# Attention's four weight products by quarters, seven for eight

## The chip, the core and the metric

The kernel runs on one core of a Trainium2 chip. A core has five engines that work side by side, each on its own queue of instructions in order: TensorE (matrix products, PE in the profile, with its weight loads as PEld), VectorE (DVE), ScalarE (ACT), GpSimd (POOL) and SyncE (SP, which here only issues DMAs). They share an on-chip memory of 128 partitions (SBUF); the matrix products land in a second memory (PSUM) of eight banks, each with 512 float32 values in every partition, and VectorE or ScalarE takes them from there. The metric is the device time of one execution in microseconds (us).

## What is computed

A layer on 4 x 2048 tokens of 256 features, all float32: linear attention with a decay inside chunks of 32 tokens, a layer norm, a gated feed-forward with integer weights, and another layer norm.

```
Q = x @ W_q.T;  K = x @ W_k.T;  V = x @ W_v.T          # D = 256, chunks of 32 tokens
decay = sigmoid(log_decay[0])
mask[i, j] = decay ** (i - j) if i >= j else 0          # 32 x 32
S = (Qc @ Kc.T) * mask;  O = S @ Vc                     # inside each chunk
out = (sigmoid(x @ W_g.T) * O) @ W_o.T + x
x = layernorm(x + out)
h = silu(x @ wg.T / 127) * (x @ wu.T / 127)             # hidden 768, integer weights
x = layernorm(x + h @ wd.T / 127)
```

The kernel uses Q K^T = x (W_q^T W_k) x^T: it forms the 256 x 256 product `m_sb` once, and per block y = x m, and then the scores from x and y. So a block of tokens meets four float32 weight matrices of 256 x 256 in attention: `m_sb`, `wg`, `wv` and `wo`.

## The kernel before

The 8192 tokens are cut into 16 blocks of 512 (`TB`). x comes in twice: transposed (`xT`, features on partitions, 2 x 128, with the 512 tokens along the row) for the products, and as it is (`xn`) for the residual. A tile that is "feature-major" has features on partitions and tokens along the row; "token-major" is the other way round, with the block's four groups of 128 tokens (`NG` = 4) side by side.

The attention of block n:
- `attn_y` (matmul L320, copy by VectorE L327) makes `yT`, feature-major: two output tiles of 128 x 512, each the sum of two products over the two halves of the features.
- `attn_gate` (L304, sigmoid by ScalarE L311) makes `sg` in the same shape.
- `attn_v` (L339, copy by ScalarE L346) makes `v`, token-major: for each group of 128 tokens two products with the 128 x 256 halves of `wv`; two groups share a bank.
- `attn_scores` (L359) forms the scores from x and y in pieces of 64 tokens, and VectorE masks them into `sT` (L369).
- `attn_values` (L380) forms the products of v and `sT`; VectorE multiplies them by the gate into `goT` (L387), feature-major.
- `attn_out` multiplies `goT` by `wo` in `project_back` (L406, named pa), VectorE adds twice x from PSUM (L427), and `layer_norm` (L264 to L288) writes h.

The feed-forward of block b then needs h feature-major and as two parts, a rounded one (`hT_hi`, float32r) and a rest (`hT_lo`, float16). `move_h` turns h by 32 x 32 transposes on VectorE (L461) and 16 small DMAs; `split_h` makes the parts on ScalarE (L484) and VectorE (L485). `ffn_up` runs over six chunks of 128 hidden features (L502): sigmoid on ScalarE (L510), two products on VectorE (L512, L514), then `u_hi` on ScalarE (L521) and `u_lo` on GpSimd (L522). `ffn_down` multiplies all of these by the weights in `project_back` (L406, named fdn), VectorE adds h (L529), and `finish` normalizes and stores.

A loop over b = 0 to 13 joins the two: the attention of block n = b + 2 stands beside the feed-forward of block b. In the order of the program: load xT and xn of n, `attn_y`, `attn_gate`, `attn_v`, `attn_scores`, `move_h` of b + 1, `ffn_up` half 0, `attn_values`, `split_h` of b + 1, `ffn_up` half 1, `attn_out` of n, `ffn_down` and `finish` of b, and a look at some of the integer weights (`look_up`, L230). Before the loop stand the attention of blocks 0 and 1, y of block 2, and the conversion of the integer weights to float32r and float16 (`integers`, L217) by ScalarE; behind it the feed-forward of the last two blocks.

The framework sets the semaphores and the queue order of each engine when the kernel is built. The order of the program gives precedence, but an instruction whose inputs are late may be passed: in the trace, the copy of `yT` stands between instructions of the layer norm of the block before. `tc.keep_in_program_order` holds single instructions to the program's order on their engine (the conversions and the split are held so). The order is fixed from then on. All eight PSUM banks belong to one pool (`bank`): a product takes a free bank and gives it back when the last reader is done.

Of the kernel before, what the change touches and what calls it, by code (L numbers as in the profile page):

```python
# [38 lines left out]
F32 = mybir.dt.float32  # L40
# [6 lines left out]
P = 128  # L47
# [4 lines left out]
NG = TB // P  # L52
SCALE = 1.0 / 127.0
# [8 lines left out]
def kernel(  # L62
# [30 lines left out]
    acts = ctx.enter_context(tc.tile_pool(name="acts", bufs=H // P + 3))  # L93
    small = ctx.enter_context(tc.tile_pool(name="small", bufs=8))
# [41 lines left out]
    if NB > 1:  # L136
        xns[1] = load_xn(1)
    ffn_int = [
        load_w(nc.sync, w, name)
        for w, name in ((ffn_gT, "fg_int"), (ffn_uT, "fu_int"), (ffn_dT, "fd_int"))  # L140
# [73 lines left out]
    def integers(w_int, name, dtype):  # L214
        name = f"{name}_{'hi' if dtype == F32R else 'lo'}"
        t = const.tile(list(w_int.shape), dtype, tag=name, name=name)
        tc.keep_in_program_order(nc.scalar.copy(t, w_int))  # L217
        return t


    halves = [
        (w_int, slice(i * w_int.shape[1] // 2, (i + 1) * w_int.shape[1] // 2))
        for w_int in ffn_int
        for i in range(2)
    ]
    top = const.tile([P, len(halves)], F32, tag="top", name="top")

    def look_up(i):
        w_int, ks = halves[i]
        reduced = nc.vector.tensor_reduce(  # L230
            top[:, i : i + 1],
            w_int[:, ks, :].rearrange("p k n -> p (k n)"),
            mybir.AxisListType.X,
            ALU.max,
            apply_absolute_value=True,
        )
        tc.keep_in_program_order(reduced)

    def count_wide():

        wide = const.tile([P, len(halves)], F32, tag="wide", name="wide")
        nc.vector.tensor_scalar(wide, top, EXACT, None, ALU.is_gt)
        ones = const.tile([P, 1], F32, tag="ones", name="ones")
        nc.vector.memset(ones, 1.0)
        pw = bank("pw")
        nc.tensor.matmul(pw[:1, : len(halves)], lhsT=ones, rhs=wide, start=True, stop=True)
        count = const.tile([1, 1], F32, tag="count", name="count")
        nc.vector.tensor_reduce(count, pw[:1, : len(halves)], mybir.AxisListType.X, ALU.add)
        n_wide = const.tile([1, 1], I32, tag="n_wide", name="n_wide")
        nc.vector.tensor_copy(n_wide, count)  # L250
        return n_wide
# [45 lines left out]

    def attn_gate(b):
        xt = xTs[b]
        sg = work.tile([P, KD, TB], F32, tag="sg", name=f"sg_{b}")  # L300
        for dc in range(KD):
            pg = bank(f"pg_{b}_{dc}")
            for ec in range(KD):
                nc.tensor.matmul(  # L304
                    pg,
                    lhsT=wg[:, ec, dc * P : (dc + 1) * P],
                    rhs=xt[:, ec, :],
                    start=(ec == 0),
                    stop=(ec == KD - 1),
                )  # L310
            nc.scalar.activation(sg[:, dc, :], pg, AF.Sigmoid)  # L311
        return sg

    def attn_y(b):
        xt = xTs[b]
        yT = work.tile([P, KD, TB], F32, tag="yT", name=f"yT_{b}")
        for fc in range(KD):
# [12 lines left out]
    def attn_v(b):  # L330
        xt = xTs[b]
        v = work.tile([P, NG, D], F32, tag="v", name=f"v_{b}")
        per = TB // D
# [40 lines left out]
    def attn_values(b, sT, v, sg):  # L374
        goT = work.tile([P, KD, TB], F32, tag="goT", name=f"goT_{b}")
        for dc in range(KD):
# [10 lines left out]
            nc.vector.tensor_tensor(goT[:, dc, :], po, sg[:, dc, :], ALU.mult)  # L387
        return goT

    def back_terms(g, parts, ws):  # L390


        pairs = list(zip(parts, ws))[:: -1 if g % 2 else 1]
        return [(part[k], w[:, k, :]) for part, w in pairs for k in range(len(part))]
# [26 lines left out]
    def attn_out(b, goT, up=H_UP):  # L421
        xn = xns.pop(b)
        r = norm.tile([P, NG, D], F32, tag="h", name=f"h_{b}")

# [6 lines left out]
        project_back(b, (chunked(goT),), (wo,), residual, "pa")  # L431
# [92 lines left out]
    def ffn_down(b, uT, h):  # L524
# [8 lines left out]
        project_back(b, uT, fd, residual, "fdn")  # L533
# [26 lines left out]
    if second:  # L560
        sT_second = attn_scores(second, ys.pop(second))
    hs[first] = attn_out(first, goT, 1 if NB == 1 else H_UP)
    fg, fu = (
        [integers(w, name, dtype) for dtype in (F32R, F16)]
        for w, name in zip(ffn_int, ("fg", "fu"))
    )
    if second:
        goT = attn_values(second, sT_second, v_second, sg_second)
    if NB > 2:
        xTs[2] = load_xT(2)  # L570
        ys[2] = attn_y(2)
    if second:
        hs[second] = attn_out(second, goT, 1 if NB == 2 else H_UP)
    fd = [integers(ffn_int[2], "fd", dtype) for dtype in (F32R, F16)]
# [5 lines left out]
    for b in range(NB - 2):  # L580
# [5 lines left out]
        uT = [], []  # L586
        yT = ys.pop(n) if n in ys else attn_y(n)
# [9 lines left out]
        if looked < len(halves):  # L597
            look_up(looked)
            looked += 1
    for i in range(looked, len(halves)):  # L600
        look_up(i)
# [70 lines left out]
    for g in range(NG):  # L672
        pb = bank(f"fdn_{last}_{g}")[:, :D]
        terms = back_terms(g, uT_last, fd)
# [31 lines left out]
    def wide_block(start, weights):  # L706
# [18 lines left out]
        for hc in range(KH):  # L725
            pg = bank(f"fg_w_{hc}")
            pu = bank(f"fu_w_{hc}")
            for pb, w in ((pg, wide_g), (pu, wide_u)):
                for dc in range(KD):
                    nc.tensor.matmul(  # L730
                        pb,
                        lhsT=w[:, dc, hc * P : (hc + 1) * P],
# [15 lines left out]
        project_back("w", (uT,), (wide_d,), residual, "fdn")  # L748
# [3 lines left out]
        n_wide, min_val=0, max_val=len(halves) * P, skip_runtime_bounds_check_because="a count"  # L752
    )
    with tc.If(wide_any > 0):
        weights = []
        for w_int in ffn_int:
            t = w_int.bitcast(F32)
            nc.vector.tensor_scalar(t, w_int, SCALE, None, ALU.mult)
            weights.append(t)
# [44 lines left out]
```

## Time and profile before

| What | Value |
|---|---|
| Time, median of 3 runs | 549.88 us (549.49 to 552.0) |
| Profiled execution: time, span | 549.92 us, 548.2 us |
| Mean granted TensorE clock | 0.995 |
| One block in the loop | 33.1 us |
| ACT_TABLE_LOAD (before sqrt and before sigmoid), each | 1283 ns |
| u_lo on POOL, 128x512 | 1280 ns |
| u on VectorE, 128x512 | 691 ns |
| sg, v on ScalarE from PSUM, 128x512 | 597, 588 ns |
| yT copy on VectorE, 128x512 | 671 ns |
| Integer conversion on ScalarE, 128x1536 | 1455 to 1470 ns |
| Largest waits: POOL for u_hi; VectorE (sT) for ps; ScalarE (s) for fg | 405.0, 78.2, 76.1 us |

The span runs from the first to the last instruction; the time is that of the device for the same execution and contains 1.7 us more. A wait in the last row is idle time of the engine that waits, in total over the span. Durations of matmuls in the groups overlap each other, so that the lengths in the chain of waits, where they don't, are the ones to add.

### The profile page before, as it was taken

To read this page: it belongs to the slowest core of one execution; us is meant where nothing else is said; L and a number is where in the kernel's file an instruction comes from. 1 tells how busy PE (TensorE), PEld (TensorE's weight loads), DVE (VectorE), ACT (ScalarE), POOL (GpSimd) and SP (SyncE) were. 2 spreads that over 40 slices of the span, in tenths; PEclk is the share of its full clock that TensorE was granted. 3 is DMA by queue.
4 is the path that set the end of the run, shared out by engine and by line. 5 is a ranking of instruction groups with operands and counts; after the bars stand their busy time and mean duration, and the time that the engine had idled before them with its cause. 6 is when DMAs were issued, how large, how long until landed. Compare 5 with 4: busy or idle time off the path is not lost.

```text
span 548.2 us, 8472 instructions
## 1 busy us (share of the span) xinstructions
PE 538.8 (98%) x3150; PEld 387.6 (71%) x3150; DVE 385.3 (70%) x956; ACT 231.3 (42%) x383; POOL 128.6 (23%) x122
## 2 busy tenths in 40 slices
PE   8999999999999999999999999999999999999994
PEld 5677767767667686677857677676676867678793
DVE  4267784859768486794848758496784858848875
ACT  2217524336243352433435243452433425344745
POOL 2000412305022040321304022050221404123453
PEclk9999999999999999999999999999999999999997
DMA  7431214121221312214122231213213120020102
GB/s 256 168 113 50 67 45 110 39 71 45 89 66 39 84 54 77 58 42 112 40 64 52 70 85 39 74 43 94 62 39 93 62 62 16 8 71 1 38 2 80
DMA packets 41996, 36.77 MB, mean 67 GB/s; under 512 B 4576, under 2 KB 37344, under 8 KB 41952
## 3 DMA queue, kind: packets, MB, share of 16 engines
q1 hardware_dynamic: 40832, 35.15, 22.5%
q10 hardware_dynamic: 1088, 1.05, 0.6%
q8 instruction: 26, 0.43, 0.3%
q14 instruction: 18, 0.15, 0.1%
q0 software_dynamic: 32, 0.00, 0.0%
HBM read 20.45 MB, written 8.39 MB: 53 GB/s over the span
## 4 chain that ended last, share of the span: by engine, by line
PE 97%; DVE 1%; ACT 1%; issue 0%; POOL 0%; DVEq 0%
PE fg L502 16%; PE fu L502 16%; PE fdn L406 15%; PE pg L304 10%; PE pa L406 10%; PE pv L339 10%; PE py L320 10%; PE po L380 5%; PE ps L359 3%; PE pi L148 1%; ACT r L646 0%; PE pt L443 0%; PE pm L162 0%; ACT L273 0%; ACT rstd_f L273 0%
## 5 line engine op out<-in xcount | busy, mean ns | idle before, releaser
L522 POOL TENSOR_TENSOR u_lo<-u,u_hi 128x512 f16<-128x512 f32 (+1 forms) x102 | 123.9, 1216 | 409.5 <-ACT u_hi L521 405.0
L510 ACT ACTIVATE s<-fg 128x512 f32<-128x512 f32 (+1 forms) x102 | 58.1, 570 | 76.2 <-PE fg L502 76.1
L512 DVE SCALAR_TENSOR_TENSOR s<-fg,s 128x512 f32<-128x512 f32 (+1 forms) x102 | 66.7, 654 | 28.0 <-ACT s L510 27.8
L521 ACT CAST u_hi<-u 128x512 fp32r<-128x512 f32 (+1 forms) x102 | 60.4, 592 | 48.8 <-DVE u L514 48.3
L514 DVE TENSOR_TENSOR u<-fu,s 128x512 f32<-128x512 f32 (+1 forms) x102 | 67.1, 660 | 13.8 <-POOL u_lo L522 1.1
L502 PE MATMUL fg<-hT_hi,fg_hi 128*128 128x512 f32 (+1 forms) x204 | 71.5, 431 | 0.0
L369 DVE TENSOR_TENSOR sT<-ps,mask 64x256 f32<-64x256 f32 x32 | 13.5, 422 | 78.5 <-PE ps L359 78.2
L502 PE MATMUL fu<-hT_hi,fu_hi 128*128 128x512 f32 (+1 forms) x204 | 61.4, 382 | 0.0
L502 PE MATMUL fg<-hT_lo,fg_lo 128*128 128x512 f16 (+1 forms) x204 | 58.9, 369 | 0.0
L304 PE MATMUL pg<-xT,wg 128*128 128x512 f32 x128 | 58.2, 598 | 0.0
L339 PEld LDWEIGHTS pv<-wv,xT 128*128 128x128 f32 x256 | 48.6, 190 | 13.4 <-issue 7.7
L502 PE MATMUL fu<-hT_lo,fu_lo 128*128 128x512 f16 (+1 forms) x204 | 58.1, 366 | 0.0
L406 PE MATMUL pa<-wo,goT 128*128 128x256 f32 x256 | 58.0, 379 | 0.0
L339 PE MATMUL pv<-wv,xT 128*128 128x256 f32 x256 | 57.9, 379 | 0.0
L320 PE MATMUL py<-xT,m_sb 128*128 128x512 f32 x128 | 57.6, 593 | 0.0
L406 PE MATMUL fdn<-fd_hi,u_hi 128*128 128x256 f32 x360 | 55.2, 295 | 0.0
L406 PEld LDWEIGHTS pa<-wo,goT 128*128 128x128 f32 x256 | 48.5, 190 | 7.6 <-DVE rstd_a L286 0.2
L406 PEld LDWEIGHTS fdn<-fd_hi,u_hi 128*128 128x128 f32 x360 | 46.6, 189 | 1.1
L304 PEld LDWEIGHTS pg<-xT,wg 128*128 128x128 f32 x128 | 24.4, 192 | 31.1 <-issue 28.9
L406 PE MATMUL fdn<-fd_lo,u_lo 128*128 128x256 f16 x360 | 44.5, 273 | 0.0
L502 PEld LDWEIGHTS fg<-hT_hi,fg_hi 128*128 128x128 f32 x204 | 36.6, 189 | 10.3
L502 PEld LDWEIGHTS fu<-hT_hi,fu_hi 128*128 128x128 f32 x204 | 37.5, 188 | 7.8
(91 smaller groups left out, 612.6 us busy)
## 6 DMA issues: line engine op xcount, KB each, us to landing
x<-in_x_dram SPq DMA_DIRECT2D x16, 512.0 KB, 3.5
xT<-in_xT_dram SPq DMA_DIRECT2D x15, 512.0 KB, 3.8
out_dram<-r SPq DMA_DIRECT2D x15, 512.0 KB, 3.3
hT<-sq SPq DMA_DIRECT2D x224, 32.0 KB, 1.9
fg_int<-in_ffn_gT_dram SPq DMA_DIRECT2D x1, 768.0 KB, 9.5
fu_int<-in_ffn_uT_dram SPq DMA_DIRECT2D x1, 768.0 KB, 10.9
fd_int<-in_ffn_dT_dram SPq DMA_DIRECT2D x1, 768.0 KB, 10.4
xT<-in_xT_dram SPq DMA_DIRECT2D x2, 256.0 KB, 4.2
```

The lines of the kernel that those rows point to most:

```text
L304: nc.tensor.matmul(pg, lhsT=wg[:, ec, dc * P : (dc + 1) * P], rhs=xt[:, ec, :], start=(ec == 0), stop=(ec == KD - 1),)
L320: nc.tensor.matmul(py, lhsT=m_sb[:, ec, fc * P : (fc + 1) * P], rhs=xt[:, ec, :], start=(ec == 0), stop=(ec == KD - 1),)
L339: nc.tensor.matmul(pv[:, j * D : (j + 1) * D], lhsT=xt[:, ec, g * P : (g + 1) * P], rhs=wv[:, ec, :], start=(ec == 0), stop=(ec == KD - 1),)
L359: nc.tensor.matmul(ps[rows, g, :], lhsT=xt[:, fc, tokens], rhs=yT[:, fc, tokens], start=(fc == 0), stop=(fc == KD - 1),)
L380: nc.tensor.matmul(po[:, cols], lhsT=v[:, g, dc * P : (dc + 1) * P], rhs=sT[:, cols], start=True, stop=True,)
L406: nc.tensor.matmul(pb[:, j * D : (j + 1) * D], lhsT=part[:, g * P : (g + 1) * P], rhs=w, start=(i == 0), stop=(i == len(terms) - 1),)
L502: nc.tensor.matmul(pb, lhsT=w[kind][:, dc, hc * P : (hc + 1) * P], rhs=hT[kind][:, dc, cols], start=(kind == kinds[0] and dc == 0), stop=( ...
L510: nc.scalar.activation(s, pg, AF.Sigmoid, scale=SCALE / H_UP)
L512: nc.vector.scalar_tensor_tensor(s, pg, U_UP / H_UP**2, s, ALU.mult, ALU.mult)
L514: nc.vector.tensor_tensor(u, pu, s, ALU.mult)
L521: nc.scalar.copy(hi, u)
L522: nc.gpsimd.tensor_tensor(lo, u, hi.bitcast(F32), ALU.subtract)
```

## The change

For blocks 2 to 15 each of the four 256 x 256 weight products is done on quarters with seven products where there were eight (Strassen's scheme in Winograd's form). The weight is cut into four quarters of 128 x 128, the block's data into four of 128 features by 256 tokens. Sums of the weight's quarters are made once by GpSimd (`weight_sums`, five small tiles for each weight), sums of the data's quarters in each block, also by GpSimd (`token_sums`: `x_sums` for y, gate and v together, `go_sums` for out). `seven` then runs the products in the order 1, 5, 7, 6 into four half-filled banks; ScalarE copies products 1, 5 and 7 out, VectorE adds 6 and 1 into `u`, GpSimd adds 5 and 7. Products 2, 3 and 4 are accumulated onto the banks of 1, 5 and 7, from which the copies were taken. The four quarters of the result are then written: one by ScalarE (c11), two by VectorE (c12, c21, bank + u), one by GpSimd (c22).

The feature-major form (y, gate) has 256 columns in a matmul where there were 512. The token-major form (v, out) has the data as the stationary operand and 128 columns where there were 256. The gate's sigmoid is applied by ScalarE after the sums, to three quarters in place. `attn_out` writes its product to SBUF, and the residual is added there from two SBUF operands.

To make room in SBUF the integer weights no longer have tiles of their own: they are loaded in nine pieces of 128 x 512 into the nine buffers of the tag `u_hi`, and ScalarE converts them in 18 instructions where there were 6. `look_up` reads the converted weights. The branch for weights beyond the exact range, which these inputs don't take, loads the integers again.

```diff
+    def weight_sums(w, name):
+        a11, a21 = w[:, 0, :P], w[:, 0, P:]
+        a12, a22 = w[:, 1, :P], w[:, 1, P:]
+        t = const.tile([P, 5, P], F32, tag=f"{name}_sums", name=f"{name}_sums")
+        s1, s2, s3, s4, minus = (t[:, i, :] for i in range(5))
+        nc.gpsimd.tensor_tensor(s1, a21, a22, ALU.add)
+        nc.gpsimd.tensor_tensor(s3, a11, a21, ALU.subtract)
+        nc.gpsimd.tensor_tensor(s2, s1, a11, ALU.subtract)
+        nc.gpsimd.tensor_tensor(s4, a12, s2, ALU.subtract)
+        nc.gpsimd.tensor_scalar(minus, a22, -1.0, None, ALU.mult)
+        return a11, a12, s4, minus, s1, s2, s3
+    def token_sums(t, name):
+        out = sums.tile([P, 4, HB], F32, tag=f"{name}_sums", name=f"{name}_sums")
+        t1, t3, t2, t4 = (out[:, i, :] for i in range(4))
+        b11, b12, b21, b22 = (t[:, k, n * HB : (n + 1) * HB] for k in range(2) for n in range(2))
+        nc.gpsimd.tensor_tensor(t1, b12, b11, ALU.subtract)
+        nc.gpsimd.tensor_tensor(t3, b22, b12, ALU.subtract)
+        nc.gpsimd.tensor_tensor(t2, b22, t1, ALU.subtract)
+        nc.gpsimd.tensor_tensor(t4, t2, b21, ALU.subtract)
+        return b11, b21, b22, t4, t1, t2, t3
+    def feature_major(a, b):
+        def product(i, pb, first):
+            nc.tensor.matmul(pb, lhsT=a[i - 1], rhs=b[i - 1],
...
+    def token_major(a, b):
+        def product(i, pb, first):
+            for g in range(HB // P):
+                nc.tensor.matmul(
+                    pb[:, g * P : (g + 1) * P],
+                    lhsT=b[i - 1][:, g * P : (g + 1) * P],
+                    rhs=a[i - 1],
+                    start=first and g == 0,
...
+    def seven(name, product, quarter, func=AF.Copy):
...
+        banks = {i: bank(f"p{i}_{name}")[:, :HB] for i in (1, 5, 7, 6)}
+        p = {}
+        for i, pb in banks.items():
+            product(i, pb, True)
+            if i != 6:
+                p[i] = part(f"p{i}")
+                nc.scalar.copy(p[i], pb)
+        u = part("p6")
+        nc.vector.tensor_tensor(u, banks[6], p[1], ALU.add)
+        p57 = part("p57")
+        nc.gpsimd.tensor_tensor(p57, p[5], p[7], ALU.add)
+        for i, onto in ((2, 1), (3, 5), (4, 7)):
+            product(i, banks[onto], False)
+        c11, c12, c21, c22 = (quarter(i, j) for i in range(2) for j in range(2))
+        nc.scalar.activation(c11, shaped(banks[1], c11), func)
+        nc.vector.tensor_tensor(c12, shaped(banks[5], c12), shaped(u, c12), ALU.add)
+        nc.vector.tensor_tensor(c21, shaped(banks[7], c21), shaped(u, c21), ALU.add)
+        nc.gpsimd.tensor_tensor(c22, shaped(p57, c22), shaped(u, c22), ALU.add)
 def attn_gate(b):
+        if b in x_sums:
+            product = feature_major(w_sums["g"], x_sums[b])
+            seven(f"g_{b}", product, by_features(sg), AF.Sigmoid)
+            for raw in (sg[:, 0, HB:], sg[:, 1, :]):
+                nc.scalar.activation(raw, raw, AF.Sigmoid)
+            return sg
 def attn_y(b):
+        if b in x_sums:
+            seven(f"y_{b}", feature_major(w_sums["m"], x_sums[b]), by_features(yT))
+            return yT
 def attn_v(b):
+        if b in x_sums:
+            seven(f"v_{b}", token_major(w_sums["v"], x_sums.pop(b)), by_tokens(v))
+            return v
 def attn_values(b, sT, v, sg):
+        if w_sums and b != "w":
+            go_sums[b] = token_sums(goT, "go")
 def attn_out(b, goT, up=H_UP):
+        if b in go_sums:
+            seven(f"o_{b}", token_major(w_sums["o"], go_sums.pop(b)), by_tokens(r))
+            for j in range(2):
+                gs = slice(j * NG // 2, (j + 1) * NG // 2)
+                nc.vector.scalar_tensor_tensor(
+                    flat(r, gs), flat(xn, gs), 2.0, flat(r, gs), ALU.mult, ALU.add
+                )
+            layer_norm(r, r, f"a{b}", on_dst=up)
+            return r
...
-    fg, fu = (
-        [integers(w, name, dtype) for dtype in (F32R, F16)]
-        for w, name in zip(ffn_int, ("fg", "fu"))
-    )
+    fg = integers(ffn_gT, ffn_int[0], "fg")
+    fu = integers(ffn_uT, ffn_int[1], "fu")
     if second:
         goT = attn_values(second, sT_second, v_second, sg_second)
     if NB > 2:
+        for w, name in ((m_sb, "m"), (wg, "g"), (wv, "v"), (wo, "o")):
+            w_sums[name] = weight_sums(w, name)
         xTs[2] = load_xT(2)
+        x_sums[2] = token_sums(xTs[2], "x")
         ys[2] = attn_y(2)
...
+        if n not in ys:
+            x_sums[n] = token_sums(xTs[n], "x")
         yT = ys.pop(n) if n in ys else attn_y(n)
```

## The prediction

> **What bounds the kernel now.** First the page: busy shares, then the chain that ended last.
>
> ```profile
> PE 538.8 (98%) x3150; PEld 387.6 (71%) x3150; DVE 385.3 (70%) x956; ACT 231.3 (42%) x383; POOL 128.6 (23%) x122
> PE 97%; DVE 1%; ACT 1%; issue 0%; POOL 0%; DVEq 0%
> ```
>
> Both say TensorE, and the second is the stronger: 97% of the span is matmuls that wait for nothing but the matmul in front. So a microsecond taken from TensorE is a microsecond of time, as long as no other engine becomes late. How much a stage really occupies I take from the chain in order of time, because there the pieces don't overlap (start, length, what). One block's stages:
>
> ```profile
> 158.75 1.78 PE po L380 x16
> ...
> 165.94 3.45 PE pa L406 x16
> 169.39 5.47 PE fdn L406 x48
> 174.86 3.43 PE py L320 x8
> 178.29 3.43 PE pg L304 x8
> 181.72 3.45 PE pv L339 x16
> ```
>
> The four products of the change are pa, py, pg, pv: 13.76 us of a block. Each float32 product is two instructions, so N=512 costs 3.43/8 = 429 ns per instruction, N=256 3.45/16 = 216, N=128 (po) 1.78/16 = 111. Cost is proportional to columns even at 128, where a weight load stands before every matmul.
>
> Then the other engines by stage (window, length, PE, PEld, DVE, ACT, POOL busy):
>
> ```profile
> 153.08:186.19 33.11, 33.11 (x196) 23.67 (x193) 24.26 (x57) 13.44 (x22) 7.67 (x6) 1.00 0.23 65
> 181.56:185.11 3.55, 3.55 (x18) 2.85 (x16) 0.00 (x0) 1.18 (x2) 0.00 (x0) 1.00 0.62 185
> 193.48:198.90 5.42, 5.42 (x27) 3.46 (x26) 5.20 (x8) 3.39 (x7) 1.76 (x2) 1.00 0.01 3
> 198.90:202.15 3.25, 3.25 (x17) 2.86 (x16) 3.02 (x6) 2.13 (x4) 2.90 (x3) 1.00 0.00 0
> ```
>
> The first line is a whole block; the others are pv, the second half of ffn_up, and pa. VectorE is not evenly loaded: 0.00 in pv, but 5.20 of 5.42 and 3.02 of 3.25 just where attn_out runs. Last, prices for half-width tiles, and one row whose time varies:
>
> ```profile
> L522 POOL TENSOR_TENSOR u_lo<-u,u_hi 128x256 f16<-128x256 f32 x12 | 8.7, 731 | 6.6 <-ACT u_hi L521 6.3
> L510 ACT ACTIVATE s<-fg 128x256 f32<-128x256 f32 x12 | 4.6, 380 | 3.3 <-PE fg L502 3.3
> L514 DVE TENSOR_TENSOR u<-fu,s 128x256 f32<-128x256 f32 x12 | 5.0, 423 | 2.2 <-POOL u_lo L522 0.9 <-PE fg L502 0.5
> L485 DVE TENSOR_TENSOR hT_lo<-hT,hT_hi x28: 677/688/1375, 63.0 to 494.4; 128x512 f16<-128x512 f32 x28
> ```
>
> hT_lo (minimum, median, maximum) has both inputs in SBUF; its long ones coincide with a u_lo on POOL.
>
> [...] a logical 512-column product takes 2 x 429 = 858 ns, a float32r one about half of one such instruction. So columns removed are paid at the full rate. [...]
>
> **The change part by part.** It acts on blocks 2 to 15, 14 of 16.
>
> TensorE. Feature-major (y, gate): 7 products x 2 instructions x 216 ns = 3.02 for 3.43, saves 0.41 each. Token-major (v, out): 7 x 2 x 2 = 28 instructions of 128 columns x 111 = 3.11 for 3.45, saves 0.34 each. Bounds of that pitch: 109 (the transposes, 8 in 0.87) and about 125, where v and out gain nothing. I take 111, the same operand shapes as po. Sum 1.50 us a block, x14 = 21.0 us. Nothing else is removed.
>
> ScalarE. Each `seven` copies three banks and writes c11: 4 x 0.38, four times 6.1; the raw sigmoids add 0.38 + 0.60; the full-width sg and v evacuations (2 x 0.60 + 2 x 0.59 = 2.4) go. Net +4.7: 13.4 to 18.1 of a block of 31.6 (57%).
>
> VectorE. Three half-width operations each, 12 x 0.42 = 5.0, less the two yT copies (1.3): +3.7, so 24.0 to 27.7 (88%). The residual of attn_out stays two operations, but now with two SBUF inputs. If they and hT_lo are always stretched by POOL (up to 0.69 each for four, less what hT_lo already pays), 29.8 (94%).
>
> POOL. x_sums 4, go_sums 4, p57 and c22 in each of four: 16 x 0.73 = 11.7, so 7.7 to 19.4 (61%).
>
> No engine passes TensorE; what decides is lateness in three places.
>
> (a) Inside a `seven`. The second wave (products 2, 3, 4) writes over banks that ScalarE must first have copied. First-wave products take 0.43 each; with 0.2 from a matmul's end to ScalarE's start (sg starts 0.2 after pg) and 0.38 a copy, p1, p5, p7 are copied at 1.0, 1.5, 1.9 us and needed at 1.7, 2.2, 2.6. Cover 0.7 us each: one 128x512 activation fits, a table load of 1.28 does not. Behind a waiting product 2 stands all of TensorE's queue. In the gate stage the load that follows the sqrt stands before c11, whose input is ready 2.4 us in, after the copies. I take 0; price if it lands earlier 0.6 us.
>
> (b) go_sums before attn_out. goT is written at 160.4 to 161.7, pa starts at 165.9: four POOL sums are 2.9, plus a u_lo 1.3, ending near 165.3, and only t1 and t3 are needed within the first microsecond. Covered, barely. They stretch both hT_lo, about 0.7 us more VectorE, in the stage where it has 0.2 spare.
>
> (c) attn_out to ffn_down. The last u_lo ends at 169.96 and fdn needs it about 1.1 into its 5.47, near 170.5: slack 0.5. With (b) the s, u, u_hi, u_lo chain is 0.7 later, attn_out is 0.34 shorter, and a p57 may stand ahead on POOL (0.73): 0.7 + 0.34 - 0.5 = 0.5 late without p57, 1.3 with it. Other ready matmuls (the next y) can fill part, if four banks are free. I take 0.45 a block, 6.5 us in all; bounds 0 and 1.3 (18 us).
>
> Banks: y and gate hold four each, all eight; v takes y's. y's u must leave before 6.2 us into the run of products; VectorE, busy with layer norms through pa and fdn and perhaps 2 us further behind than now, does it near 4. Covered.
>
> Prologue. The casts go from 6 of 128x1536 (1.37 apart) to 18 of 128x512 (0.52 apart): +1.1 us on ScalarE, which is full from 38.5 to 53.6. They are ordered early, so the copies of block 2's y and gate queue behind them, and TensorE waits for those copies now. pa of block 1 and the transposes (4.3 us) hide most of the first wait; the fd casts delay the gate's. I take 2 us, bounds 0 and 6. weight_sums: 16 sums of about 0.45 and 4 scalings, some 8.5 us on POOL, which is idle from 4.3 to 58.3: free. The split integer loads land before 38: free. The branch for wide integers isn't taken: free.
>
> Sum against the profiled execution: 549.92 (span 548.2, 1.7 around it) - 21.0 + 6.5 + 2 = 537.4. The median of the three runs is 549.88, the same within 0.04. Forecast **537.5 us**.
>
> **Rivals.**
> R1, all hidden: (c) and the prologue cost under 2 us together: 549.9 - 21 + 1 = 530. For it: before, TensorE waits nowhere in a block. Against: (c)'s slack is 0.5.
> R2, weight loads set the pitch of the token-major products: at 125 ns v and out gain nothing; 549.9 - 14 x 0.82 + 8.5 = 547. For it: 16 more loads a block at full rate. Against: po runs so at 111.
> R3, slower: the POOL and VectorE chain before ffn_down. If p57, c22 and two sums of x stand in front of the last u_lo (4 x 0.73 = 2.9) on top of 0.5, TensorE stops 3.0 us a block after partial filling: 549.9 - 21 + 42 + 2 = 573; with half of it filled, 552. It decides from 1.4 us a block on ((21 - 2)/14). For it: VectorE at 88 to 94% and in order; a late r or bank release has the same price. Against: POOL is idle 39%, and nearly all added VectorE work can fall in the pv stage.
> R4, the products are not shortened (second waves serialised behind ScalarE by 0.6 us each): 4 x 0.6 x 14 = 34, less 21: 563, also slower.
>
> **How the numbers follow.** Forecast (531.5 to 543) 0.50; R1 0.12; R2 or larger stalls, 543 to 549, 0.09 (0.08 of it below 547.2); R3 0.19; R4 0.05; stalls that just cancel the gain, 0.05. The likeliest one's own range is 531.5 to 543. The range 528 to 556 leaves out the far part of R3 and R4. What this kernel's measurement can tell is about 0.5%, 2.7 us: faster 0.70, same 0.06, slower 0.24.
>
> **What would show it.** Right: per block about 31.6 + 0.45 us; pv and pa pieces near 3.1, py and pg near 3.0; VectorE 27 to 30 a block; a TensorE gap before fdn waiting for u_lo, and one in 40 to 55 us waiting for ScalarE. Wrong: gaps before second-wave products with ScalarE as releaser in every `seven` (R4); matmul pitch above 120 ns at 128 columns (R2); VectorE idle only where TensorE idles too (R3).

## The result, and the profile after

The changed kernel is slower: 587.81 us (585.3 to 588.79, 4 runs) against 550.76 us for the kernel before on the same chip, a ratio of 1.0666 [1.0621, 1.071]. (The median for the kernel before is of four runs; the table above has three of them.) The forecast was 537.5 us with a range up to 556. Later runs found that the loss hangs on where one step stands in the loop: with that step moved and all four products still by seven, it takes 542.59 us. A version with three more edits, one of which gives attn_out its eight products back, takes 536.25.

First the page of the changed kernel: busy shares (microseconds, share of the span, instructions), then the engines' shares of the chain that ended last.

```profile
PE 538.2 (92%) x3654; PEld 430.2 (73%) x3654; DVE 444.9 (76%) x1096; ACT 284.0 (48%) x591; POOL 300.7 (51%) x366
PE 34%; DVE 22%; SPq 20%; ACT 8%; issue 6%; DMA 5%; POOL 5%; DVEq 0%; ACTq 0%
```

TensorE's share of the chain fell from 97% to 34%, and 20% belongs to a queue that the prediction prices nowhere: SPq, SyncE issuing transfers (DMAs). The span grew by 37.8 us (548.2 to 586.0): 3.2 before the loop, 29.5 in 13 block periods (from one block's scores to the next; 2.27 each, where 1.05 less was forecast), 5.2 in the last block and behind the loop.

One block by the windows view (window, length, then PE, PEld, DVE, ACT, POOL busy):

```profile
159.74:194.61 34.87, 32.61 (x233) 26.46 (x229) 28.61 (x68) 17.28 (x36) 19.14 (x23) 1.00 0.23 61
```

VectorE (27 to 30 forecast), ScalarE (18) and GpSimd (19) carry about what the prediction gave them, and none is full. The seven products are as short as forecast too: in the timeline y's first starts at 184.26 and the gate's first at 187.28, 3.02 us later. The time is in TensorE's pauses: over the span it idles 47.8 us (586.0 - 538.2), where it was 9.4 before. The waits view (engine, line, waited for: total us, times, longest) names the largest of them, and two more:

```profile
ACT hT_hi L637 <- DMA hT<-sq: 28.3, 13, 2.9
DVE hT_lo L638 <- ACT hT_hi L637: 25.6, 12, 2.7
PEld p_o L378 <- ACT p_o L404: 20.3, 20, 1.8
PE p_o L378 <- ACT p_o L404: 16.5, 20, 1.6
PEld L549 <- POOL u_lo L675: 11.3, 13, 1.7
PE fdn L549 <- POOL u_lo L675: 6.8, 5, 1.4
```

The last four are TensorE: before the second wave of attn_out (p_o) and before ffn_down (fdn); the PEld lines are the same pauses seen by the weight loads, so they aren't added to the PE lines. The first two are no wait of TensorE, and the most instructive: once a block, 13 times, ScalarE stands still for h of the next block, and 12 times VectorE behind it. Before, the same row (its last fields are idle time ahead of it and the releaser) had next to none; the first line is the kernel before, the second the changed one:

```profile
L485 DVE TENSOR_TENSOR hT_lo<-hT,hT_hi 128x512 f16<-128x512 f32 x28 | 26.9, 1000 | 0.9 <-ACT hT_hi L484 0.8
```
```profile
L638 DVE TENSOR_TENSOR hT_lo<-hT,hT_hi 128x512 f16<-128x512 f32 x28 | 26.2, 974 | 28.6 <-ACT hT_hi L637 25.6
```

Why hT comes late is in the timeline. Before (start, length, what), y of the next block began at 174.70:

```profile
175.64 0.43 DVE L461 STREAM_TRANSPOSE sq<-h 128x256 f32<-128x256 f32 x1
...
178.14 0.43 DVE L461 STREAM_TRANSPOSE sq<-h 128x256 f32<-128x256 f32 x1
...
181.19 8.53 SPq L467 DMA_DIRECT2D hT<-sq  x13
...
194.19 1.14 ACT L484 CAST hT_hi<-hT 128x512 fp32r<-128x512 f32 x2
```

The four transposes of h end 3.9 us after y's start, SyncE issues 16 transfers until 189.72, the last lands 1.9 later at 191.6, and ScalarE splits hT at 194.19 without waiting: 2.6 us to spare. After, y began at 149.40; the chain of waits of that stretch (pieces of up to 0.05 us are left out):

```profile
157.19 0.33 DVE p_g L406
157.52 0.06 DVE sq L614
...
157.80 0.39 DVE sg L413
158.21 0.34 ACT sg L434
158.56 0.24 issue
158.80 0.63 ACT sg L434
159.43 0.42 SPq L620
...
168.36 0.59 SPq L620
169.00 1.87 DMA hT<-sq
170.97 0.63 ACT hT_hi L637
171.62 0.59 DVE hT_lo L638
...
173.23 0.60 DVE u L667
...
175.28 0.63 ACT u_hi L674
175.91 0.07 issue
175.98 1.08 POOL u_lo L675
177.06 0.17 issue
177.22 0.74 POOL p_o L408
177.96 0.07 issue
178.03 0.72 POOL h L415
178.75 1.23 POOL u_lo L675
180.03 4.41 PE fdn L549 x37
```

The transposes now stand between the additions of y, gate and v on VectorE; the timeline has the last at 158.77 to 159.19, and its end is 9.8 us after y's start. That is 5.9 later than before, and 2.6 were to spare. About half of it comes from those additions. Where they are there and attn_out has its eight products (the run e2 below), y of the same block starts at 143.95 and the last transpose is

```profile
150.35 0.43 DVE L612 STREAM_TRANSPOSE sq<-h 128x256 f32<-128x256 f32 x1
```

It ends 6.8 us after y's start, 3.0 later than before. The other 3.0 come with attn_out by seven: its norm writes h until 152.45, 3.0 us after y's start (149.40), where before it was done 0.3 us after (174.99 against 174.70).

SyncE's issues follow the last transpose (159.25 to 169.60; the chain names the gate's sigmoid as the last releaser on the way, but the first issue is 0.06 us behind the transpose). Then come the landing and the split; behind the split, in the fixed order of ScalarE and VectorE, stand the sigmoids, products and u_hi of the block's last chunks, then GpSimd's u_lo, and only then ffn_down, whose residual and norm stand ahead of the next transposes on VectorE. So it is a ring from block to block: lateness in one block is handed to the next. Nothing in this block's ffn_down needs hT of the next block: this link of the ring is a place in two queues and no data.

A transfer of 32 KB lands 1.9 us after its issue (the median of all 224; 1.87 for the last one above). What counts here is the time on the issuing queue: 0.59 us on SyncE for most of them and 0.04 between two, one behind the other, 10.35 us for 16.

### The profile page after: what moved, and what is told of

Read it like the earlier page. It is cut to its first block, busy times and chain, and to the rows that moved or that the text cites. A ratio compares the mean times of both kernels' runs of the same rounds, so it can differ in the third digit from the quotient of the medians.

```text
span 586.0 us, 10552 instructions
## 1 busy us (share of the span) xinstructions
PE 538.2 (92%) x3654; PEld 430.2 (73%) x3654; DVE 444.9 (76%) x1096; ACT 284.0 (48%) x591; POOL 300.7 (51%) x366
## 3 DMA queue, kind: packets, MB, share of 16 engines
q10 hardware_dynamic: 1088, 1.05, 0.5%
## 4 chain that ended last, share of the span: by engine, by line
PE 34%; DVE 22%; SPq 20%; ACT 8%; issue 6%; DMA 5%; POOL 5%; DVEq 0%; ACTq 0%
SPq L620 20%; PE fdn L549 12%; DMA hT<-sq 4%; PE p_y L362 4%; DVE hT_lo L638 4%; DVE u L667 4%; POOL u_lo L675 3%; DVE r L318 3%; PE p_o L378 3%; DVE s L665 3%; DVE h L318 2%; PE p_g L362 2%; PE fg L655 2%; PE fu L655 2%; PE p_v L378 2%
## 5 line engine op out<-in xcount | busy, mean ns | idle before, releaser
L408 POOL TENSOR_TENSOR p_y<-p_y,p_y 128x256 f32<-128x256 f32 x14 | 11.4, 814 | 93.0 <-ACT p_y L404 93.0
L549 PE MATMUL fdn<-fd_lo,u_lo 128*128 128x256 f16 x360 | 47.5, 277 | 7.7 <-POOL u_lo L675 6.8
L638 DVE TENSOR_TENSOR hT_lo<-hT,hT_hi 128x512 f16<-128x512 f32 x28 | 26.2, 974 | 28.6 <-ACT hT_hi L637 25.6
L549 PEld LDWEIGHTS <-u_lo 128*128 128x128 f16 x360 | 32.1, 99 | 16.2 <-POOL u_lo L675 11.3
L378 PE MATMUL p_o<-o_sums,go_sums 128*128 128x128 f32 x224 | 35.0, 289 | 3.4 <-DVE s L665 1.3
L303 ACT ACTIVATE rstd_a<-mv_a,eps 128x4 f32<-128x4 f32 x16 | 4.8, 297 | 64.4 <-DVE mv_a L295 64.4
L572 DVE SCALAR_TENSOR_TENSOR h<-x,h 128x512 f32<-128x512 f32 x28 | 24.4, 910 | 15.1 <-POOL h L415 15.1
L655 PEld LDWEIGHTS <-fu_lo 128*128 128x128 f16 x204 | 19.9, 98 | 21.5
L378 PEld LDWEIGHTS p_o<-o_sums,go_sums 128*128 128x128 f32 x224 | 29.8, 198 | 6.1 <-issue 6.0
```

Source lines behind the costliest of these rows:

```text
L378: nc.tensor.matmul(pb[:, g * P : (g + 1) * P], lhsT=b[i - 1][:, g * P : (g + 1) * P], rhs=a[i - 1], start=first and g == 0, stop=True, ski ...
L549: nc.tensor.matmul(pb[:, j * D : (j + 1) * D], lhsT=part[:, g * P : (g + 1) * P], rhs=w, start=(i == 0), stop=(i == len(terms) - 1),)
L638: rest = nc.vector.tensor_tensor(in_order[1], whole, in_order[0].bitcast(F32), ALU.subtract)
L655: nc.tensor.matmul(pb, lhsT=w[kind][:, dc, hc * P : (hc + 1) * P], rhs=hT[kind][:, dc, cols], start=(kind == kinds[0] and dc == 0), stop=( ...
```

## The experiments

The median of the kernel before lay between 550.3 and 550.9 us beside all of these runs. In the expectations T1 and T2 are the first two theories; L1 (the loop theory) is the ring described above, in which they meet.

### First split: late turn of h (T1) or attn_out by seven (T2)

*e1* moves the transposes and transfers ahead of the next block's y; *e2* lets attn_out have eight products; *e3* does both.

```diff
 # e1, e3
+        moving = move_h(b + 1, hs[b + 1])
         if n not in ys:
...
         sT = attn_scores(n, yT)
-        moving = move_h(b + 1, hs[b + 1])
 # e2, e3
-        if w_sums and b != "w":
-            go_sums[b] = token_sums(goT, "go")
```

> The changed kernel with move_h placed ahead of attn_y in the loop, so that VectorE makes the four transposes before the sums of y, gate and v; nothing else. Theory T1 (the transposes come 6 us later because y's, the gate's and v's additions stand ahead of them, the 16 DMAs that SyncE issues behind them need 10.4 us plus 1.9 to land, and split_h then blocks ScalarE and VectorE): the DMAs start about 4 us earlier or more, the waits of hT_hi for the DMA (28.3 us in all) go below 3 us, attn_out's product falls from 4.7 to 6.7 us to 3.1 to 3.6, a block takes 32 to 33 us; time 550 to 563. T2 (attn_out by seven products overloads VectorE, ScalarE and GpSimd between ffn_up and ffn_down whatever the transposes do): time 580 to 588.

> The changed kernel with attn_out by eight products as before (no go_sums, no seven for out), y, gate and v by seven; move_h where it was. T1: transposes still stand behind the sums of y, gate and v, hT is still late by 1 to 2 us, so 2 us a block stay lost; time 555 to 575. T2: the cause is gone with attn_out's sums, a block takes 31.9 to 32.3 us; time 538 to 546.

> Both edits: move_h ahead of attn_y, and attn_out by eight products. T1: no stall left in the loop; y and gate save 0.41 us each and v 0.34, 14 times 1.16 = 16 us, less about 4 us that the prologue lost; time 536 to 543. T2: the same as e2_out_eight within 2 us.

Measured: e1 573.55, ratio 1.0416 [1.0394, 1.0438], between both theories; e2 543.29, 0.9858 [0.9837, 0.9879], as T2 said; e3 548.3, 0.996 [0.9948, 0.9972], which neither had: T1 expected 536 to 543, T2 e2's time within 2 us. The waits view of e1 has none for hT left, and in their place

```profile
PEld p_v L378 <- DVE yT L413: 15.3, 13, 1.4
PE p_v L378 <- DVE yT L413: 12.9, 13, 1.2
```

v takes over banks that y held, and VectorE, with the transposes ahead, reads one of them late. So turning first trades one wait for another. What e3 loses against e2 was not followed up. In e2 the chain is TensorE at 93%, and a block takes 32.10 us with no pause (windows view):

```profile
218.60:250.70 32.10, 32.10 (x220) 26.30 (x216) 25.84 (x65) 16.21 (x32) 15.03 (x17) 1.00 0.24 66
```

Attn_out by seven thus costs 44.5 us in this order; whether by its work or by its timing was open. Two runs left out single parts of its work on GpSimd.

```diff
 # e7
-            go_sums[b] = token_sums(goT, "go")
+            go_sums[b] = b11, b21, b22, b11, b12, b21, b22
 # e8, for attn_out only
-        nc.gpsimd.tensor_tensor(p57, p[5], p[7], ALU.add)
...
-        nc.gpsimd.tensor_tensor(c22, shaped(p57, c22), shaped(u, c22), ALU.add)
+            nc.scalar.copy(c22, shaped(p[7], c22))
```

> The changed kernel with the four sums of goT's quarters left out: attn_out's seven products take plain quarters in their place, so that its output is another one; everything else, the order too, stays. L1 (attn_out's quarters arrive in one lump at the end, its layer norm starts 4 us later, and so do the transposes and the 16 DMAs: a loop from block to block that these sums are only a small part of): 4 to 12 us are won, time 575 to 584. L2 (GpSimd's added work, which stretches VectorE's two-input instructions and stands ahead of u_lo, is the cost): time 552 to 566.

> The changed kernel without GpSimd's two additions in attn_out (p57 and c22): ScalarE copies product 7 into the fourth quarter instead, so that its output is another one. L1: the residual needs no GpSimd and starts about 0.9 us earlier and u_lo has nothing of out ahead of it, but the layer norm still starts late; time 566 to 580. L2: with go_sums still there but u_lo's place ahead restored, 550 to 564.

Measured: 579.35, 1.0531 [1.0504, 1.0559], and 571.41, 1.039 [1.0358, 1.0422]. Taken away singly, these sums give back 8.5 and 16.4 us, both in L1's ranges; but the waits for hT stay (26.5 and 26.7 us), and so neither part of the work is the cause by itself. Both left out together was not run.

### The lateness alone

*e4* is the kernel before with its transposes held behind the masks of the scores, and nothing added. *e11* is e2 with attn_out's two residual additions turned about and held in that order, so that the norm begins when the whole product is there, as it does with seven products.

```diff
 # e4
+            masked = nc.vector.tensor_tensor(
...
+            turned = nc.vector.transpose(
...
+                tc.keep_in_program_order(turned)
 # e11
         project_back(b, (chunked(goT),), (chunked(wo),), residual, "pa")
+        for gs, pb in halves[::-1]:
+            added = nc.vector.scalar_tensor_tensor(
```

> The kernel before, with the four transposes of move_h held behind the masks of attn_scores on VectorE from the second turn of the loop on; nothing of the seven products. T1: transposes move from about 3.8 to about 12.5 us after the start of the block's products, hT lands near 25 us in, the split stands ahead of the last chunk's products on VectorE, u_lo comes 1 to 3 us late for ffn_down; 13 blocks lose 1 to 2.5 us each; time 563 to 583. T2: the lateness of the transposes is covered; time 549 to 553.

> Attention's y, gate and v by seven, attn_out by eight, with attn_out's residual additions turned about: the second half of the product first, so that no layer norm starts before the whole product is there, as when seven products give all quarters at the end (nothing is added or left out). L1 (the late sum of attn_out moves all that follows on VectorE, and the ring has no slack left): 1 to 2 us a block lost, 553 to 572. Rival (the cost of attn_out by seven is its extra work and the waits inside it, the lump is harmless): 542 to 546.

Measured: e4 605.73, 1.1013 [1.0979, 1.1047], a loss beyond even T1's range, on a kernel without a single product by seven; its chain shows SPq at 20%, as the changed kernel's. Not all of these 55 us are waiting. TensorE is busy for 561.1 us with the same products that took 538.8 before, and the granted clock fell to 0.965 (0.995 before). It falls in ffn_down, behind the pause (1.80 us here; windows view, one ffn_down; the columns as above, then the granted clock, the DMA share and GB/s):

```profile
178.50:185.23 6.73, 6.61 (x42) 5.45 (x43) 4.03 (x18) 1.57 (x2) 1.28 (x1) 0.75 0.24 80
```

In the kernel before, the clock of 169.00 to 174.80, with an ffn_down in it, was 1.00. So some 18 to 22 of the 55 us are matmuls that ran slower behind the pauses. This is an estimate: the clock lost over the span is 21.1 us (0.035 x 603.6) against 2.7 before, and the busy time is 22.3 more. What is left, some 33, would lie within T1's range.

e11 568.15, 1.0315 [1.0275, 1.0355], in L1's range: a mere change of order costs 25 us, and the two waits are back, once a block:

```profile
DVE hT_lo L641 <- ACT hT_hi L640: 32.7, 13, 4.1
ACT hT_hi L640 <- DMA hT<-sq: 31.3, 13, 4.0
```

### The link through SyncE

*e9* (changed kernel) and *e10* (e4) issue the 16 transfers from two queues by turns.

```diff
-                nc.sync.dma_start(
+                (nc.sync, nc.scalar)[j % 2].dma_start(
```

> The changed kernel, with the 16 transfers of hT issued by turns from SyncE's queue and from ScalarE's. Loop theory (L1): the span has a ring from block to block in which SyncE's 10.4 us of issue is one link; hT_hi then starts 4 to 5 us earlier, the waits of ScalarE and VectorE on hT go, and the time is 560 to 576, although ScalarE pays some 8 issues a block. Rival (VectorE's load and the late sum of attn_out alone set the pace, the transfers only fill idle time): no gain, or ScalarE's added issues make it slower, 583 to 592.

> The kernel before with its transposes held behind the masks of the scores, as in the run that did this before (605.7), and the 16 transfers by turns from SyncE's and ScalarE's queues. L1: the transposes are late by themselves, but the ring is shorter by some 5 us, more than the 4.4 us a block lost: most of the 55 us goes, 553 to 580. Rival (the late transposes hurt by VectorE's order, not through SyncE): 598 or more.

Measured: e9 596.78, 1.0834 [1.0804, 1.0864], beyond the rival's range; e10 591.51, 1.0731 [1.07, 1.0762], between. e9 doesn't tell what it was made for. ScalarE's timeline in it:

```profile
236.95 5.16 ACTq L620 DMA_DIRECT2D hT<-sq  x8
242.16 1.09 ACT L663 ACTIVATE s<-fg 128x512 f32<-128x512 f32 x2 [5.01 <-DMA hT<-sq]
```

The eight issues fill ScalarE's queue for 5 us just ahead of the block's first sigmoid of ffn_up: the time is taken from SyncE and put onto an engine of the ring. The split's wait did go (VectorE's for hT_hi is 4.3 us in all where it was 25.6), but the issues hold up the sigmoids for 69.0 us in all, and TensorE's wait for attn_out's copies grew from 16.5 to 24.8. Three runs change SyncE's part alone: *e13* issues four transfers twice, *e14* moves the same bytes by eight transfers, into permuted places, *e15* does so in e11.

```diff
 # e13
+                for _ in range(2 if b > 1 and q == NQ - 1 else 1):
 # e14, e15
+        for q in range(0, NQ, 2):
...
+                    hT[j * SQ : (j + 1) * SQ, :, q : q + 2, :].rearrange(
```

> The changed kernel with the last four of the 16 transfers of hT issued twice in each block from the third on, with the same data: 2.4 us more on SyncE's queue (4 x 0.6) and nothing on any other engine. L1 (SyncE's issue is a link of the ring from block to block): 13 blocks x 2 to 2.4 us more, 608 to 621. Rival (the transfers have slack, VectorE and ScalarE set the pace): 585 to 592.

> The changed kernel with hT moved by 8 transfers of 64 KB where there were 16 of 32 KB: the bytes are the same, but the 32-wide pieces land in permuted places, so the feed-forward computes with another hT. SyncE's issue is 5 us shorter and no engine has more to do. L1: the ring is 5 us shorter, more than the 3.8 us a block that the kernel loses, until the next bound (the waits inside attn_out, the late u_lo): 548 to 572. Rival: 580 to 590.

> The version with attn_out by eight and its residuals turned about (568.2 when it ran), with the same 8 transfers of 64 KB in permuted places. L1 (the lump costs what it costs because the ring has no slack for it): nearly all of it goes, 540 to 550. Rival (the lump costs by itself, on VectorE): 560 to 570.

Measured: e13 598.62, 1.0868 [1.0841, 1.0894], slower by 10.8 us, between the rival's range and L1's, which expected 20 or more; e14 563.43, 1.0245 [1.0227, 1.0262]; e15 544.63, 0.9904 [0.9887, 0.9922], within 1.3 us of e2. Five microseconds less on SyncE give back 24.4 and 23.5 us, and e14's list of waits names hT no more. The late sum of attn_out costs 25 us when the 16 transfers take 10.4 us of issuing, and 1.3 when the 8 take about 5.2 (half of that, since each takes 595 ns in the median, as each of the 16 did): in this order it costs next to nothing by itself.

Why 2.4 us more on the same link cost only 0.8 a block shows in e13's timeline. The queues were ordered anew when it was built, and the split came to stand further back. In the changed kernel all three products u of ffn_up's second half, and all three u_hi, come behind the split; in e13, in 11 blocks, one u and two u_hi do. The link got longer, and what hangs on it shorter. So e13 says less on SyncE's price than it was made for, and an edit that touches one engine can move work on another.

### Opening the ring

The split of hT stood ahead of the second half of ffn_up. *e16* moves it behind attn_out in the changed kernel, and no other line changes.

```diff
-        hTs[b + 1] = split_h(b + 1, moving)
         ffn_up(b, hT, uT, half[1])
         hs[n] = attn_out(n, goT, 1 if n == NB - 1 else H_UP)
+        hTs[b + 1] = split_h(b + 1, moving)
```

> The changed kernel with the split of hT (ScalarE's hT_hi and VectorE's hT_lo) moved behind attn_out in the loop, where it stood ahead of the second half of ffn_up. Nothing is left out. L1: hT is not needed by this block's ffn_down at all, it only stands in the queues ahead of the work that is; with the split behind that work the ring through SyncE's transfers is open, and what is left are the copies, the late u_lo and the sum of attn_out: 555 to 572. Rival (VectorE's and GpSimd's load sets the pace): 582 to 592.

Measured: 542.59, 0.9865 [0.9838, 0.9892]: 45.2 us less than the changed kernel, well past L1's 555 to 572. L1 had kept the copies, the late u_lo and the sum of attn_out as losses of their own; they went along. Its chain, one block in order of time (ffn_up's pieces left out):

```profile
201.19 5.51 PE fdn L549 x48
206.69 3.23 PE p_y L362 x14
209.93 3.02 PE p_g L362 x14
212.95 3.30 PE p_v L378 x28
216.25 1.08 PE ps L500 x32
...
222.93 1.78 PE po L521 x16
...
230.11 3.12 PE p_o L378 x28
233.24 5.52 PE fdn L549 x48
```

It holds nothing but TensorE, 32.05 us from one ffn_down to the next. The turn of h is no earlier: in the next block the transposes end at 252.71, 14.1 us after y's start at 238.59, and SyncE issues until 263.56. It is late and harmless, since the split now comes at 271.53, behind the work that ffn_down needs.

The 45.2 us are more than the lateness of hT alone. In e14 nothing waits for hT any more, TensorE's wait for attn_out's copies is 4.5 us instead of 16.5 and that for u_lo 0.4 instead of 6.8, and it gains 24.4 us. The other 20.8 lie between e14 and e16. e16 moved not only a wait but the split's own work, out of the stretch in which attn_out's copies and the last u_lo are due, and out of GpSimd's way (e14, then e16):

```profile
L641 DVE TENSOR_TENSOR hT_lo<-hT,hT_hi 128x512 f16<-128x512 f32 x28 | 35.0, 1289 | 0.2
```
```profile
L638 DVE TENSOR_TENSOR hT_lo<-hT,hT_hi 128x512 f16<-128x512 f32 x28 | 17.9, 679 | 0.0
```

It isn't that VectorE has less to do: it is busy for 442.4 us in e16 and 444.9 in the changed kernel. How the 20.8 us divide between the place of this work and its stretching was not measured.

### What is left, and a faster version

Four edits on the way to a better order: *e5* is e2 with the third block's y, gate and v by eight as well; *e12* adds the order v, y, gate; *e17* adds the later split; *e18* is e17 with attn_out by seven. *e6* moves the feed-forward's norm behind the scores, in e1.

```diff
 # e5, e12, e17, e18
-        x_sums[2] = token_sums(xTs[2], "x")
 # e12, e17, e18
+        v = attn_v(n)
         yT = ys.pop(n) if n in ys else attn_y(n)
-        sg, v = attn_gate(n), attn_v(n)
+        sg = attn_gate(n)
 # e6
-        finish(b, ffn_down(b, uT, hs.pop(b)))
+        r_b = ffn_down(b, uT, hs.pop(b))
+        later = b, r_b, norm_stats(r_b, f"f{b}", H_UP)
```

> e2_out_eight with block 2 by eight products too: y, gate and v by seven from block 3 on. Theory P1 (the prologue lost 5.6 us in e2 because block 2's second-wave products wait for copies that stand behind ScalarE's 18 conversions): the stalls at 45 and 50 us go, 1.16 us of saving is given up; time 537 to 541. P2 (the conversions themselves are later by being 18 instructions, whatever waits on them): time 542 to 546.

> e1_turn_first (all four products by seven, transposes first) with the last step of the feed-forward's layer norm, its store and look_up moved behind attn_scores of the next turn: 2.3 to 3 us of VectorE work leave the place ahead of y's additions. D1 (what is left in e1 is order on VectorE: y's banks come free late because that work stands ahead, and v waits for them, 28 us in all): the wait of p_v for yT goes; time 548 to 560. D2 (VectorE has too much work from attn_out to y altogether): the stall moves, time 566 to 575.

> The version with attn_out by eight and seven products from the fourth block on, with the order v, y, gate of the products in a block where it was y, gate, v. If what is left of the stalls is v's copies behind the gate's sigmoids on ScalarE: 536 to 540. If v's place beside ffn_down's end or the banks cost more: 540 to 546.

> The version with attn_out by eight, seven products from the fourth block on and the order v, y, gate (539.3 when it ran), with the same move of the split. L1: the few waits for hT that are left there go, 536 to 539.5; if the split now delays ffn_down's additions or the norm: 540 to 548.

> All four products by seven (y, gate and v from the fourth block on, attn_out from the third), the order v, y, gate, and the split of hT behind attn_out. Against the version with attn_out by eight (536.3 when it ran) 14 blocks x 0.34 us of matmuls are less: 530 to 534 if attn_out's additions are now covered by other work (L1); 536 to 543 if VectorE, at 82% of the span with all four by seven, or the late sum of attn_out takes it back.

| Run | us | ratio to before |
|---|---|---|
| e5 | 540.26 | 0.9809 [0.9793, 0.9825] |
| e6 | 566.09 | 1.0272 [1.0253, 1.0291] |
| e12 | 539.27 | 0.9787 [0.9761, 0.9812] |
| e17 | 536.25 | 0.9745 [0.9719, 0.9771] |
| e18 | 551.06 | 1.0015 [1.0005, 1.0025] |

e6 took away e1's bank wait, as its first theory said, and left small ones, but with 7.5 us gained its time is that of the second. e5 shows the price of the third block in the prologue: 3.0 us come back, although the 1.16 us that its products save are given up. e12's interval overlaps e5's, so its order shows no gain by itself. e17 is the fastest of the study, 2.55% below the kernel before. e18 missed both ranges: with v in front, y comes second, nearer to the scores, and its waits view has

```profile
PE ps L500 <- DVE yT L414: 13.1, 13, 1.5
```

Here attn_out's late sum does cost. Its residual and norm stand on VectorE ahead of y's additions, and the scores wait for those; in e16 y comes first, and no such wait is left. Whether e16 with the third block by eight beats e17 was not run.

## Why the prediction was wrong

**The shorter products: right.** y and gate were put at 3.02 us, v and out at 3.11. e16's chain has 3.23 (y), 3.02 (gate), 3.30 (v) and 3.12 (out), with some pauses in it. R2 is out, and so is R4: with the ring open, its pauses in every `seven` aren't there.

**The step that failed** is "what decides is lateness in three places". There was a fourth: move_h's transposes behind the new additions on VectorE, SyncE's 16 transfers behind them, and the split that stood in ScalarE's and VectorE's queues ahead of the block's own work. The change touches no line of it. But the prediction itself added 3.7 us to VectorE and expected it "perhaps 2 us further behind", and it weighed that lateness against y's banks alone, not against the transposes on the same queue: they came 5.9 us later, on a slack of 2.6, half of it behind the additions of y and gate and half with attn_out's later norm. The split's place was worth 45.2 us (e16), of which the lateness of hT was 24.4 (e14). With the split behind, the same four products by seven take 542.59 us, inside the forecast's own 531.5 to 543, at its upper edge.

**(c), attn_out to ffn_down: mis-sized as a consequence.** It was taken at 0.45 us a block with bounds of 0 and 1.3; the loop lost 3.8 (2.27 slower, although 1.50 of products were taken out). Its u_lo did come late, with p57 and c22 in front as R3 supposed (177.22 and 178.03 in the chain). But e8, which left both out, gave back only 16.4 us, and e16 with both in place waits there for 1.0 us at most in the whole span. With the ring open the block takes 32.05 us, just the 31.6 + 0.45 of the forecast, but that is luck: the 0.4 us lie in y's and v's products, where (a) took nothing, and not before ffn_down. (0.45 for 14 blocks is 6.3 us, where the sum has 6.5.)

**(a) was nearly right about its own cover and wrong about its condition.** The 0.7 us hold only while ScalarE is free to copy; in the changed kernel attn_out's copies stood behind the waiting split, 16.5 us of TensorE's time. **(b)** named a true effect, that go_sums stretch hT_lo (1289 ns in e14, 679 away from them in e16), and called it covered. In the closed ring go_sums were worth 8.5 us (e7); no wait of TensorE in e16 names them. VectorE's load, put at 24.0 us a block before, is 24.26 in the line shown there, which changes nothing.

**Banks, "Covered".** This held in the changed kernel, where no wait of TensorE names y's additions, and failed in e1, where v waits 12.9 us for y's bank.

**Prologue**: 2 us were taken, bounds 0 and 6. TensorE waits there 1.2 us for y's and 2.6 for the gate's copies behind ScalarE's conversions, 3.8 together, in the place that was forecast. The term was under-sized within its bounds.

**The rivals.** R3 had the side right, but named a chain that cost a part of the loss; its 573 was exceeded, and the ring is longer than GpSimd's queue. All-hidden R1 (530) was not reached by any order tried.

## What to carry to other kernels

When work is added to an engine, follow everything that stands behind it in that engine's queue, through the transfers that it releases and into the queue where their result is awaited, even if none of these lines is changed. A wait placed ahead of work that doesn't need it was free here while it had 2.6 us of slack (the two engines of the split waited 1.5 us in all), and closed a ring once it had none (53.9 us): put the consumer of a slow transfer behind the current block's own work. Taking out parts of the added work one by one gives each a share of the loss that none of them owns; shortening a link of the ring, and opening it, told more. And compare the order of the queues before and after an edit: it can change where no line was touched.

## What the runs showed of the hardware

VectorE's application of the norm, an operation with one tensor in SBUF, took longer beside GpSimd too; the prediction left it out of the stretched work. Before and after:

```profile
L288 DVE TENSOR_SCALAR h<-h,mv_a,rstd_a 128x256 f32<-128x256 f32 x64 | 21.9, 405 | 0.1
```
```profile
L318 DVE TENSOR_SCALAR h<-h,mv_a,rstd_a 128x256 f32<-128x256 f32 x64 | 27.9, 497 | 0.1
```

In the changed kernel 44 of the 64 have no work of GpSimd beside them and take 397 to 414 ns; the other 20 take 405 to 916, 703 in the mean. In its chain, the application that runs beside GpSimd's sum of p_y (151.40 to 152.30) takes 0.82 us. In e1 the feed-forward's norm reached a mean of 593 ns (398 before). What the two engines contend for, no run shows.

GpSimd's sums were stretched in turn. Where go_sums ran beside hT_lo (e1), its first two sums took a mean of 1180 and 1175 ns, against 735 for the other two, and hT_lo 1288. Their starts lie as far apart: twice 1.14 us in one block (from 240.27 us), then 0.81. In e16 hT_lo has moved away from GpSimd's sums and takes 676 to 684 ns in all 28 places. The stretching moved in part to other work: in one block (from 246.10 us) the four applications of the feed-forward's norm take 2.19 us together, beside two of GpSimd's sums, where one block of the changed kernel has 1.68 (from 154.64).

Pauses of TensorE cost more than their length in e4. Behind those that end at 141.91, 178.52 and 216.57 us (2.44, 1.80 and 2.44 long), twelve matmuls of fd_lo and u_lo take 2.75, 2.81 and 2.78 us, and the next twelve of them in the same ffn_down 1.49, 1.48 and 1.48; the second of these ffn_downs is the one shown above at a mean granted clock of 0.75. Behind a pause of 1.63 us, which ends at 253.22, the first twelve take 1.66 in two pieces. What decides between them was not followed up.
